# Cross-attention values by seven block products, with the context laid in another order

## The chip, the cores and the metric

The kernel runs on one core of one Trainium2 chip. The metric is the device time of one execution in microseconds (us). All data are float32.

## The reference, cut to what matters

The reference is one decoder layer: self attention, cross attention and a feed-forward network (FFN), each behind a layer norm and with a residual sum. There are 16 batches of 112 tokens with 512 features, 16 heads of 32, and a context of 375 tokens a batch.

```python
q = proj(hs, Wq, bq, S); k = proj(at, Wk, bk, T); v = proj(at, Wv, bv, T)
scores = clip(einsum('bhsd,bhtd->bhst', q, k) / sqrt(32), -50, 50)
scores = where(attend, scores, -10000.0); scores = clip(scores, -50, 50)
probs = softmax(scores); ctx = einsum('bhst,bhtd->bhsd', probs, v)
delta = clip(residual_scale, 0, 0.3) * (ctx @ Wo.T + bo); x = x + layernorm(delta)*gamma + beta
```

The change touches `k` and `v` of this cross attention: the products of the context (375 x 512) with two 512 x 512 weights.

## The kernel before, in words

`decoder_layer` (L1842) runs `finite_layer`, and after it `general_layer`, a slow version, only if a flag says that some value wasn't finite or in bounds. All below is in `finite_layer`.

**Stages.** Self attention (about 0 to 327 us), cross attention (327 to 826 us) and the FFN (826 to 1368 us). In the first two, a fixed chain of attention steps is interleaved with "pieces" of matrix products: a `Filler` `f` holds generators, each `yield` of a generator says how many us its matmuls are thought to take, and `f.fill(us)` issues pieces until so many us are used up. TensorE's order is the order in which the program issues its instructions (`manual_schedule`, L1610). The order on the other engines is made by a scheduler when the program is built.

**Cross attention.** The loop at L1699 goes over 16 batches `b`, and inside over three thirds (`kc`) of 125 context tokens. One `Cross.step` (L1238) does: 16 score matmuls (keys by queries), exponentials `e` on ScalarE, the weighting of the step before by its values (`weigh`), sums of `e` over the thirds on VectorE (`es`, L1280), and after the last third the sum over keys on TensorE (L941), four reciprocals and a product on VectorE (`divide`, L1284). Then `f.fill` issues pieces that prepare batch `b + 1`: its values, its keys, each second batch the queries of two batches (L870 ff., `xq`), and, once in four batches, output projections (`AfterCross`, L1188) whose finishing work is done on VectorE in the three batches that follow.

**Context, keys, values.** `Keys(b)` (L1066) loads one batch's context, features on partitions, as one DMA of 128 x 4 x 375 into a buffer `cT`. `sums` forms four block differences `kt` of it on VectorE. `keys` makes the keys by Strassen's scheme in Winograd's form: context and weights are cut into 2 x 2 blocks, and seven block products take the place of eight. The products share three PSUM banks and partly accumulate into each other; VectorE adds the results and the bias. `values` makes three tiles of 125 tokens x 512, each with four matmuls of 512 columns (`token_rows`, L887) and one copy on VectorE (L897). In the loop the two are interleaved: `mixed(values, keys, 2)`.

**Buffers.** PSUM tag `mm` has three banks in this stage: the products of values, keys, queries, projections and the key sums of `divide` rotate through them. The tag `big` has four buffers, shared by `cT` and `kT`; `v` has five; `w` (weights, `kt`, FFN blocks `f`) has eight; `row` has four, and holds among others the mask `mi` (L752) and the normalised rows `xn` (L789) at the start.

**The mask.** `mask_t` has 125 rows and 48 columns (batch by third). POOL loads it and makes scale and bias of the exponentials, `scl`, `nscl`, `bia`.

Of the kernel before, what the change touches and what calls it, by code (L numbers as in the profile page):

```python
# [12 lines left out]
I32 = mybir.dt.int32  # L13
U8 = mybir.dt.uint8
AF = mybir.ActivationFunctionType
ALU = mybir.AluOpType
AX = mybir.AxisListType

P = 128
# [7 lines left out]
KC = 3  # L27
# [570 lines left out]
def finite_layer(  # L598
# [47 lines left out]
    def weight(name):  # L646
        return wt.tile([P, C, D], F32, tag="w", name=name)
# [10 lines left out]
    def row(name):  # L658
        return ln.tile([P, D], F32, tag="row", name=name, bufs=4)
# [89 lines left out]
    nc.gpsimd.tensor_tensor(rs2, rs, rs, ALU.mult)  # L749


    mi = row("mi").bitcast(I32)[:KP, : B * KC]  # L752
    nc.gpsimd.dma_start(out=mi, in_=mask_t)
    scl, nscl, bia = (keep.tile([KP, B * KC], F32, name=n) for n in ("scl", "nscl", "bia"))
    nc.gpsimd.tensor_scalar(scl, mi, 0.5, SCALE, op0=ALU.is_gt, op1=ALU.mult)
    nc.gpsimd.tensor_scalar(nscl, scl, -1.0, None, op0=ALU.mult)
    nc.gpsimd.tensor_scalar(bia, mi, 0.5, 50.0, op0=ALU.is_gt, op1=ALU.mult)
    nc.gpsimd.tensor_scalar(bia, bia, -50.0, None, op0=ALU.add)

    dbk = keep.tile([P, 2], F32, name="dbk")  # L760
# [182 lines left out]
            )  # L943


    class Group:


# [7 lines left out]
        def keys(self):  # L956
            self.k = big("kT")
            yield from features(self.k, wk, xyT[:, :, ts(self.g, GT)], GT)
# [76 lines left out]
            f.drain()  # L1035

    def s_sums(s, a11, a12, a21, a22):
        for k, x0, x1, op in (
            (0, a21, a22, ALU.add),
            (1, s[:, 0], a11, ALU.subtract),
            (2, a11, a21, ALU.subtract),
            (3, a12, s[:, 1], ALU.subtract),  # L1050
        ):
            nc.vector.tensor_tensor(s[:, k], x0, x1, op)

    def t_sums(t, b11, b12, b21, b22):

        for k, x0, x1 in (
            (0, b12, b11),
            (1, b22, t[:, 0]),
            (2, b22, b12),
            (3, b21, t[:, 1]),  # L1060
        ):
            nc.vector.tensor_tensor(t[:, k], x0, x1, ALU.subtract)

    HK = (S2 + 1) // 2

    class Keys:  # L1066


        def __init__(self, b):
            self.b, self.v = b, []  # L1070
            self.c = big("cT")
            nc.sync.dma_start(out=self.c[:, :, :S2], in_=ctx_t[b])
            nc.gpsimd.memset(self.c[:, :, S2 : 2 * HK], 0.0)

        def sums(self):
            self.t = weight("kt").rearrange("p c n -> p (c n)")[:, : 8 * HK].rearrange(
                "p (s k n) -> p s k n", s=4, k=2
            )
            self.bs = [
                self.c[:, ts(d, 2), ts(k, HK)] for d in range(2) for k in range(2)  # L1080
            ]
            t_sums(self.t, *self.bs)

        def first_keys(self):
            self.k = big("kT")
            yield from features(self.k, xk, self.c[:, :, :S2], S2, bk)

        def keys(self):


            self.k = big("kT")
            c11, c12, c21, c22 = (
                self.k[:, ts(d, 2), ts(k, HK)] for d in range(2) for k in range(2)
            )
            b11, b12, b21, b22 = self.bs
            (a11, a12, a21, a22), s, t = xk_blocks, xks, self.t

            def bank():
                return psum("mm", [P, D])[:, : 2 * HK].rearrange("p (m n) -> p m n", m=2)

            def product(acc, lhs, rhs, first):
                for m in range(2):
                    for k in range(2):
                        nc.tensor.matmul(  # L1104
                            acc[:, m],
                            lhs[:, k, ts(m, P)],
                            rhs[:, k],
                            start=first and m == 0 and k == 0,
                            stop=k == 1,
                            skip_group_check=True,  # L1110
                        )
                return 1.28

            add, st = nc.vector.tensor_tensor, nc.vector.scalar_tensor_tensor
            a = bank()
            took = product(a, a11, b11, True)
            for m in range(2):
                nc.vector.tensor_scalar(
                    c21[:, m], a[:, m], bk[:, 2 + m : 3 + m], None, op0=ALU.add
                )  # L1120
            yield took
            b = bank()
            took = product(b, s[:, 1], t[:, 1], True)
            for m in range(2):
                st(
                    c12[:, m],
                    in0=b[:, m],
                    scalar=dbk[:, m : m + 1],
                    in1=c21[:, m],
                    op0=ALU.add,  # L1130
                    op1=ALU.add,
                )
            yield took
            took = product(a, a12, b21, False)
            for m in range(2):
                nc.vector.tensor_scalar(
                    c11[:, m], a[:, m], bk[:, m : m + 1], None, op0=ALU.add
                )
            yield took
            took = product(b, s[:, 2], t[:, 2], False)  # L1140
            add(c22, b, c21, ALU.add)
            yield took
            d = bank()
            took = product(d, s[:, 0], t[:, 0], True)
            add(c22, d, c22, ALU.add)
            yield took
            took = product(b, a22, t[:, 3], False)
            add(c21, b, c21, ALU.add)
            yield took
            took = product(d, s[:, 3], b22, False)  # L1150
            add(c12, d, c12, ALU.add)
            yield took

        def values(self, kcs=range(KC)):
            for kc in kcs:
                v = values("v")
                self.v.append(v)
                yield from token_rows(
                    v[:KP], xv, self.c[:, :, ts(kc, KP)], nc.vector.tensor_copy
                )  # L1160

    class Queries:

# [67 lines left out]
    class Cross:  # L1231
# [5 lines left out]

        def step(self, b, kc, q, keys, f, us):  # L1238
            scs = scores(
                lambda i, j: keys.k[ds(i * DH, DH), j, ts(kc, KP)],  # L1240
                lambda i, j: q[ds(i * DH, DH), j, ts(b % 2, S)],
                KP,
            )
            n = b * KC + kc
            late = self.late

            es = [(pair("es", "es", 3) if kc == 0 else pair("e"))[:KP] for _ in scs]
            self.late = (b, kc, keys.v[kc][:KP], es)
            for i, sc in enumerate(scs):
                nc.scalar.activation(  # L1250
                    es[i], sc, AF.Exp, scale=scl[:, n : n + 1], bias=bia[:, n : n + 1]
                )
            for i, sc in enumerate(scs):
                nc.scalar.activation(  # L1254
                    sc,
                    sc,
                    AF.Relu,
                    scale=nscl[:, n : n + 1],
                    bias=limit[:KP, :1],
                    accum_out=low[:KP, 2 * n + i : 2 * n + i + 1],  # L1260
                )
            self.weigh(late)
            for i in range(2):
                self.add(late, i)
            self.divide(late)
            f.fill(us)
# [10 lines left out]
        def add(self, late, i):  # L1277
            if late is not None and late[1] > 0:
                total = self.es[i][:KP]
                self.last = nc.vector.tensor_tensor(  # L1280
                    total, total, late[3][i][:KP], ALU.add
                ).ins

        def divide(self, late):  # L1284
            if late is not None and late[1] == KC - 1:
# [385 lines left out]
    for _ in w2_prep:  # L1671
# [6 lines left out]
    kv.append(Keys(0))  # L1678
    lay(11, 15.5, mixed(grp[3].values(range(GB)), n2[1].transposes(), 5))

    xks = weight("xks").rearrange("p c n -> p (c n)").rearrange(
        "p (s k n) -> p s k n", s=4, k=2
    )
    xk_blocks = [
        xk[:, ts(k, 2), ts(d, 2 * P)] for d in range(2) for k in range(2)
    ]
    s_sums(xks, *xk_blocks)
    lay(12, 10.5, after_self(whole[2], n2[2]))
    lay(13, 10, n2[2].ahead(False), kv[0].first_keys())
    kv.append(Keys(1))  # L1690
    lay(14, 12, mixed(kv[0].values(), n2[2].transposes(), 3))
    qs = [Queries(n) for n in range(B // 2)]
    lay(15, 9.5, qs[0].pieces(), output_bias())
# [5 lines left out]
    for b in range(B):  # L1699
# [16 lines left out]
        if b + 1 < B:  # L1716


            f.add(mixed(kv[b + 1].values(), kv[b + 1].keys(), 2))
            if b % 2:  # L1720
                queries = qs[(b + 1) // 2].pieces()
                us += 6.0
                if bl == 3 and g < 3:
                    n = n2[3] if g == 0 else n3[g - 1]
                    queries = mixed(queries, n.transposes(), 6)
                    us += 2.0
                f.add(queries)
# [170 lines left out]
```

## Time and profile before

| | us |
|---|---|
| three runs | 1371.20, 1369.81, 1370.17 (median 1370.17) |
| the profiled execution | 1369.86 |
| its span in the profile | 1368.1 |
| TensorE (PE) busy | 1347.5 |
| TensorE's weight loads (PEld) busy | 805.2 |
| VectorE (DVE) busy | 788.3 |
| ScalarE (ACT) busy | 462.0 |
| GpSimd (POOL) busy | 35.4 |

A line of a group names the source line, the engine, the operation, output<-inputs by the program's names, the shapes and the count; then busy time in us and the mean ns of one; then the idle time of the engine just before them and what ended it. A line of a timeline has start, length, engine, line, operation, names, count, and in brackets the idle time before it and who ended it. Matmuls are pipelined, and their ends are modelled: two that follow each other overlap in the profile, so what one costs is the distance between starts. One float32 matmul of the source appears as two records.

### The profile page before, as it was taken

What the parts mean: (1) busy time and instruction counts of PE and PEld (TensorE: products, weight loads), DVE (VectorE), ACT (ScalarE), POOL (GpSimd) and SP (SyncE); (2) the same over time, 40 slices, a digit from 0 to 9 for tenths busy, and PEclk for the clock granted to TensorE, in tenths of its full rate; (3) what the DMA queues carried; (4) which work ended last, traced back from release to release, by engine and by line L of the source; (5) the groups of instructions that cost most, each with busy time, mean ns of one, the idle gap of its engine ahead of it and who ended that gap; (6) DMA issues with size and microseconds to landing.
All of it is one profiled execution on the core that took longest, in us unless ns stands there. A gap on an engine that the chain in (4) does not pass through costs nothing.

```text
span 1368.1 us, 20027 instructions
## 1 busy us (share of the span) xinstructions
PE 1347.5 (98%) x8328; PEld 805.2 (59%) x8328; DVE 788.3 (58%) x1509; ACT 462.0 (34%) x901; POOL 35.4 (3%) x68
## 2 busy tenths in 40 slices
PE   8999999999999999999999999999999999999997
PEld 5555555556676767766777765544555555555554
DVE  3377987783645575547655567557654245554332
ACT  3355664553344435343445453201110011111000
POOL 2000001030000100000000000000000000000000
PEclk9999999999999999999999999999999999999999
DMA  9100002610000000000011011112031112322201
GB/s 319 52 1 16 17 15 86 245 54 1 23 24 24 31 24 23 24 24 24 24 39 39 25 48 32 46 31 62 31 123 62 47 61 69 93 65 89 93 0 56
DMA packets 59720, 74.02 MB, mean 54 GB/s; under 512 B 2641, under 2 KB 47713, under 8 KB 57317
## 3 DMA queue, kind: packets, MB, share of 16 engines
q1 hardware_dynamic: 57952, 69.44, 15.4%
q0 software_dynamic: 672, 1.62, 0.5%
q8 instruction: 67, 1.10, 0.3%
q10 hardware_dynamic: 996, 1.59, 0.3%
q14 instruction: 33, 0.26, 0.1%
HBM read 61.63 MB, written 11.01 MB: 53 GB/s over the span
## 4 chain that ended last, share of the span: by engine, by line
PE 91%; DVE 5%; ACT 1%; DMA 1%; issue 1%; POOL 0%; ACTq 0%; SPq 0%; DVEq 0%; POOLq 0%
PE mm L892 15%; PE gate L1462 12%; PE mm L874 10%; PE mm L1104 9%; PE ys L1462 7%; PE mm L903 7%; PE gate L1396 6%; PE mm L1462 5%; PE sc L919 5%; PE ys L930 4%; PE ys L1396 4%; PE mm L1396 3%; PE sc L1027 2%; PE mm L835 1%; PE mm L941 1%
## 5 line engine op out<-in xcount | busy, mean ns | idle before, releaser
L892 PE MATMUL mm<-xv,cT 128*125 128x512 f32 x384 | 178.6, 601 | 0.0
L1250 ACT ACTIVATE e<-sc,bia,scl 125x896 f32<-125x896 f32 x64 | 68.4, 1094 | 192.1 <-PE sc L919 192.1
L892 PEld LDWEIGHTS mm<-xv,cT 128*125 128x125 f32 x384 | 68.4, 187 | 75.5 <-issue 74.1
L1254 ACT ACTIVATE sc<-sc,limit,nscl 125x896 f32<-125x896 f32 x96 | 102.6, 1068 | 0.0
L1462 PE MATMUL gate<-t,f 128*128 128x448 f32 x256 | 101.4, 539 | 0.0
L1280 DVE TENSOR_TENSOR es<-es,e 125x896 f32<-125x896 f32 x64 | 68.4, 1089 | 52.5 <-ACT e L1250 52.5
L1396 PE MATMUL gate<-h,f 128*128 128x448 f32 x224 | 86.6, 539 | 0.0
L1462 PE MATMUL gate<-xyT,f 128*128 128x448 f32 x192 | 80.1, 540 | 0.0
L994 ACT ACTIVATE e<-sc,mx 112x112 f32<-112x112 f32 x256 | 64.4, 399 | 42.5 <-DVE mx L990 42.5
L1462 PE MATMUL ys<-t,f 128*128 128x448 f32 x192 | 77.4, 539 | 0.0
L1462 PEld LDWEIGHTS gate<-t,f 128*128 128x128 f32 x256 | 48.6, 190 | 47.6 <-issue 47.0
L1478 ACT COPY u<-gate 128x448 f32<-128x448 f32 x16 | 8.5, 531 | 182.3 <-PE gate L1462 109.4
L1104 PEld LDWEIGHTS mm<-kt,xks 128*128 128x128 f32 x360 | 59.0, 190 | 15.3 <-issue 14.9
L1396 PEld LDWEIGHTS gate<-h,f 128*128 128x128 f32 x224 | 42.5, 190 | 41.3 <-issue 40.9
L1292 DVE RECIPROCAL r<-mm 128x112 f32<-128x112 f32 x64 | 47.8, 810 | 30.8 <-PE mm L941 30.8
L1104 PE MATMUL mm<-kt,xks 128*128 128x188 f32 x360 | 63.5, 324 | 0.0
L989 DVE TENSOR_REDUCE mx<-sc 112x8 f32<-112x896 f32 x32 | 33.6, 1083 | 42.4 <-PE sc L919 42.4
L892 PE MATMUL mm<-wv,xyT 128*112 128x512 f32 x128 | 58.0, 596 | 0.0
L1462 PEld LDWEIGHTS ys<-t,f 128*128 128x128 f32 x192 | 36.5, 190 | 35.7 <-issue 35.5
L1408 DVE TENSOR_TENSOR h<-h,h 128x896 f32<-128x896 f32 x32 | 32.8, 1084 | 40.9 <-PE ys L1396 31.7
L1462 PEld LDWEIGHTS gate<-xyT,f 128*128 128x128 f32 x192 | 36.0, 190 | 34.4 <-issue 33.7
L919 PE MATMUL sc<-q,kT 32*125 32x112 f32 x1536 | 54.7, 279 | 0.0
(211 smaller groups left out, 2192.8 us busy)
## 6 DMA issues: line engine op xcount, KB each, us to landing
f<-in_f_w SPq DMA_DIRECT2D x64, 256.0 KB, 3.1
f<-blocks SPq DMA_DIRECT2D x14, 1024.0 KB, 4.8
cT<-in_ctx SPq DMA_DIRECT2D x16, 750.0 KB, 4.8
w<-in_f_w SPq DMA_DIRECT2D x4, 1024.0 KB, 10.3
blocks<-w SPq DMA_DIRECT2D x4, 1024.0 KB, 5.4
xr<-in_x SPq DMA_DIRECT2D x2, 1024.0 KB, 10.8
out_y<-o SPq DMA_DIRECT2D x8, 256.0 KB, 3.2
xr<-in_x SPq DMA_DIRECT2D x2, 768.0 KB, 15.7
```

What stands on the lines that cost most here:

```text
L874: nc.tensor.matmul(acc[:, :n], w[:, c, ts(j, P)], src[:, c, :], start=(c == 0), stop=(c == C - 1))
L892: nc.tensor.matmul(acc[:n, :], src[:, c, :], w[:, c, :], start=(c == 0), stop=(c == C - 1))
L903: nc.tensor.matmul(acc, xyT[:, c, ts(t, P)], w[:, c, :], start=(c == 0), stop=(c == C - 1))
L919: nc.tensor.matmul(views[i // 2][:, i % 2, j, :], k_of(i, j), q_of(i, j), start=True, stop=True)
L930: nc.tensor.matmul(y[ts(i, DH), j, :], v[:, HG * j + i, :], es[i // 2][:n, i % 2, j, :], start=first and j == 0, stop=last, skip_group_che ...
L994: nc.scalar.activation(e[:, i, j, :], sc[:, i, j, :], AF.Exp, scale=SCALE, bias=mx[:, i, j : j + 1],)
L1104: nc.tensor.matmul(acc[:, m], lhs[:, k, ts(m, P)], rhs[:, k], start=first and m == 0 and k == 0, stop=k == 1, skip_group_check=True,)
L1250: nc.scalar.activation(es[i], sc, AF.Exp, scale=scl[:, n : n + 1], bias=bia[:, n : n + 1])
L1254: nc.scalar.activation(sc, sc, AF.Relu, scale=nscl[:, n : n + 1], bias=limit[:KP, :1], accum_out=low[:KP, 2 * n + i : 2 * n + i + 1],)
L1280: self.last = nc.vector.tensor_tensor(total, total, late[3][i][:KP], ALU.add).ins
L1396: nc.tensor.matmul(banks[m][bank], o[:, c, ts(m, P)], t[:, c, :], start=first and c == 0, stop=c == UNITS - 1, skip_group_check=True,)
L1462: nc.tensor.matmul(bank, o[:, s, k, :], t[:, k, :], start=first and k == 0, stop=k == 1, skip_group_check=True,)
```

## The change

1. **Context in another order.** The load is split into five DMAs. Tokens 0 to 124 stand at columns 0 to 124, tokens 125 to 249 at columns 188 to 312, and the last 125 fill what is left of the two halves of 188 columns (63 and 62); the first 63 of these are laid a second time at the end (columns 375 to 437), so that each third is also one run of columns (`third`). The memset of the padding goes.
2. **Two thirds of the values by seven products** (`Seven.rows`): the tiles of tokens 0 to 249 come from seven products of two matmuls with 256 columns, with the weight's block sums `xvs` (made once) and the block sums `kt` that the keys use already. Each product has a bank; VectorE makes eight sums of 125 x 256. The last third stays a direct product, and is issued first.
3. **Keys with a bank for each product** (`Seven.biased`): the same seven products in another order, with no accumulation across products, and one more sum on VectorE. After them POOL copies 63 columns of the keys to the end of the tile (`whole`).
4. **Mask.** The mask is loaded a second time in two parts, into a second `row` buffer, for the order of the last third, and scale and bias of that third are made from it.
5. Batch 0 keeps direct keys (376 columns instead of 375) and direct values, from the new layout.

```diff
-    mi = row("mi").bitcast(I32)[:KP, : B * KC]
-    nc.gpsimd.dma_start(out=mi, in_=mask_t)
-    nc.gpsimd.tensor_scalar(scl, mi, 0.5, SCALE, op0=ALU.is_gt, op1=ALU.mult)
-    nc.gpsimd.tensor_scalar(bia, mi, 0.5, 50.0, op0=ALU.is_gt, op1=ALU.mult)
+    parted = (S2 + 1) // 2 - KP
+    for kcs, parts in (
+        (slice(0, KC), ((0, 0, KP),)),
+        (slice(KC - 1, KC), ((0, parted, KP - parted), (KP - parted, 0, parted))),
+    ):
+        mi = row("mi").bitcast(I32)[:KP, : B * KC]
+        for to, start, n in parts:
+            nc.gpsimd.dma_start(out=mi[ds(to, n)], in_=mask_t[ds(start, n)])
+        m, sc_, bi = (
+            t.rearrange("p (b k) -> p b k", k=KC)[:, :, kcs] for t in (mi, scl, bia)
+        )
+        nc.gpsimd.tensor_scalar(sc_, m, 0.5, SCALE, op0=ALU.is_gt, op1=ALU.mult)
+        nc.gpsimd.tensor_scalar(bi, m, 0.5, 50.0, op0=ALU.is_gt, op1=ALU.mult)
...
+        def biased(self, dst, src, t, bias, over):
...
+            acc = product(a11, b11)
+            for m in range(2):
+                nc.vector.tensor_scalar(
+                    c21[:, m], acc[:, m], bias[:, 2 + m : 3 + m], None, op0=ALU.add
+                )
+            yield took
+            add_over(c11, product(a12, b21), c21)
+            yield took
+            add(c12, product(s[:, 1], t[:, 1]), c21)
+            yield took
+            add(c22, product(s[:, 2], t[:, 2]), c12)
+            yield took
+            add(c21, product(a22, t[:, 3]), c22)
+            yield took
+            acc = product(s[:, 0], t[:, 0])
+            add(c22, acc, c22)
+            add(c12, acc, c12)
+            yield took
+            add_over(c12, product(s[:, 3], b22), c12)
+            yield took
+
+        def rows(self, dst, src, t):
...
+            for w, x, *sums in (
+                (a11, b11, (c21, None)),
+                (a12, b21, (c11, c21)),
+                (s[:, 1], t[:, 1], (c12, c21)),
+                (s[:, 2], t[:, 2], (c22, c12)),
+                (a22, t[:, 3], (c21, c22)),
+                (s[:, 0], t[:, 0], (c22, c22), (c12, c12)),
+                (s[:, 3], b22, (c12, c12)),
+            ):
+                acc = psum("mm", [P, D])[:n, : 2 * P]
+                for k in range(2):
+                    nc.tensor.matmul(acc, x[:, k, :n], w[:, k], start=k == 0, stop=k == 1)
+                for c, more in sums:
+                    if more is None:
+                        nc.vector.tensor_copy(c, acc)
+                    else:
+                        nc.vector.tensor_tensor(c, acc, more, ALU.add)
+                yield 0.9
...
-            nc.sync.dma_start(out=self.c[:, :, :S2], in_=ctx_t[b])
-            nc.gpsimd.memset(self.c[:, :, S2 : 2 * HK], 0.0)
+            self.x = self.c[:, :, : 2 * HK]
+            parted = HK - KP
+            for to, start, n in (
+                (0, 0, KP),
+                (KP, 2 * KP, parted),
+                (HK, KP, KP),
+                (HK + KP, 2 * KP + parted, KP - parted),
+                (S2, 2 * KP, parted),
+            ):
+                nc.sync.dma_start(
+                    out=self.c[:, :, ds(to, n)], in_=ctx_t[b][:, :, ds(start, n)]
+                )
+
+        @staticmethod
+        def third(ap, kc):
+            return ap[..., ds(min(kc, 1) * HK + max(kc - 1, 0) * KP, KP)]
+
+        def whole(self):
+            nc.gpsimd.tensor_copy(self.k[:, :, S2 : HK + 2 * KP], self.k[:, :, KP:HK])
...
+        def pieces(self):
             self.k = big("kT")
+            keys = xks.biased(self.k, self.x, self.t, bk, dbk)
+            self.v = [values("v") for _ in range(2)]
+            rows = xvs.rows(
+                [v[:KP].rearrange("p h r -> p (h r)") for v in self.v],
+                quarters(self.x),
+                self.t,
+            )
+            last = self.third_of_values(KC - 1)
+            for _ in range(2):
+                yield next(last)
+            for _ in range(7):
+                yield next(rows)
+                yield next(keys)
+            self.whole()
...
+    xvs = Seven("xvs", xv)
...
-            f.add(mixed(kv[b + 1].values(), kv[b + 1].keys(), 2))
+            f.add(kv[b + 1].pieces())
```

## The prediction

> **What bounds the kernel now.** I read the busy times first, then the busy times of the stretch of cross attention (326.6 to 826.0 us, columns: length, then busy time and count of PE, PEld, DVE, ACT, POOL, then clock, DMA share, GB/s).
>
> ```profile
> PE 1347.5 (98%) x8328; PEld 805.2 (59%) x8328; DVE 788.3 (58%) x1509; ACT 462.0 (34%) x901; POOL 35.4 (3%) x68
> ```
> ```profile
> 0.00:40.00 40.00, 33.73 (x155) 22.61 (x156) 15.61 (x61) 12.14 (x24) 8.97 (x30) 1.00 0.86 291
> 326.60:826.00 499.40, 497.48 (x4737) 350.28 (x4736) 291.90 (x537) 230.68 (x354) 6.92 (x18) 1.00 0.09 27
> ```
>
> TensorE leaves 1.9 of 499.4 us idle there, at a granted clock of 1.00, so this stretch is worth what its matmuls take. The mean of a group (592 to 601 ns for 512 columns) isn't that price: matmuls overlap. The pitch is. In the timeline of the weight loads, and in the chain's whole runs (start, length, count):
>
> ```profile
> 635.25 0.19 PEld L892 LDWEIGHTS mm<-xv,cT 128*125 128x125 f32 x1 [0.24 <-issue]
> 635.68 0.19 PEld L892 LDWEIGHTS mm<-xv,cT 128*125 128x125 f32 x1 [0.24 <-issue]
> ```
> ```profile
> 658.18 6.05 PE mm L874 x32
> ...
> 1021.97 6.01 PE mm L1396 x16
> ```
>
> One record of 512 columns comes each 0.429 us, one of 448 each 6.01/16 = 0.376, one of 224 each 6.05/32 = 0.189. The line through these is 0.833 ns a column plus 2.5 ns. It gives 0.216 for 256 columns, which lie between two measured widths. Every fp32 matmul of the source is two records (64 calls of 16 score matmuls are 1,536 plus 512 records).
>
> **The term on the path: the values.** For each of batches 1 to 15, two of three value tiles (8 matmuls, 16 records of 512) go, and seven products of 2 matmuls (28 records of 256) come. 16 x 0.429 = 6.87 us; 28 x 0.216 = 6.05. That is 0.82 a batch, **-12.3 us** in all. The keys keep 28 matmuls of 188 columns. Bounds: -12.9 (exactly 7/8 of the columns) to 0, should the pitch not hold.
>
> The trace speaks against this pitch nowhere. The Trainium skill does (TensorE: Matmul & The Clock Gate, "Back-to-back issue gap"): it measures streams at 81 ns for 128 columns and 131 for 512, so width costs little. As an estimate by that page, 256 columns cost 98/131 of 512, the new products 28 x 0.321 = 9.0 us, and the kernel would be 2.1 us a batch, 32 us in all, slower. The rows above, 0.189 at 224 and 0.429 at 512, don't agree with it.
>
> **What VectorE gets.** Durations by row: 0.42 for 128x256, 0.55 for 128x376, 0.41 for 128x188 (two in a row 0.73), 0.69 for a 125x512 copy.
>
> ```profile
> L1280 DVE TENSOR_TENSOR es<-es,e 125x896 f32<-125x896 f32 x63 | 67.3, 1089 | 51.5 <-ACT e L1250 51.5
> L1292 DVE RECIPROCAL r<-mm 128x112 f32<-128x112 f32 x60 | 44.8, 810 | 30.8 <-PE mm L941 30.8
> L1141 DVE TENSOR_TENSOR kT<-mm,kT 128x376 f32<-128x376 f32 x15 | 8.2, 547 | 5.2 <-PE mm L1104 5.2
> L1052 DVE TENSOR_TENSOR f<-f 128x256 f32<-128x256 f32 x8 | 3.0, 421 | 3.0 <-DMA f<-in_f_w 3.0
> ```
>
> A batch loses two copies (1.38) and gains eight 256-wide sums (3.4 alone, 2.9 in a row) and one 376-wide key sum (0.5): +2.0 to 2.5 us on 18.2, where a batch has some 31. So VectorE goes from 59% to about 67%: not the bound by its sum. What counts is **how soon it empties a bank**. The values and keys had 6 banks a batch out of 3; now 15 products take one each, about every 1.07 us (0.86 for rows, 1.28 for keys). A product waits when VectorE is more than two products (2.14 us) behind. In the trace of before nearly all evacuations start 0.04 to 0.7 us after their matmul, but behind the sums `es` or the reciprocals up to 2.5 us. Before, this cost little:
>
> ```profile
> 636.41 2.98 DVE L1292 RECIPROCAL r<-mm 128x112 f32<-128x112 f32 x4
> 639.30 0.63 DVE L897 COPY v<-mm 125x512 f32<-125x512 f32 x1
> 639.54 1.51 PE L1104 MATMUL mm<-cT,xk 128*128 128x188 f32 x8 [0.69 <-DVE r L1292]
> ```
>
> Here (batch 8 to 9) the sums of the softmax hold one of the three banks until the reciprocals end, 8.7 us after the scores began at 630.71, since finishing work on `xr` stood ahead of them. Matmuls covered 1.07 + 0.80 + 0.86 + six of 512 (5.3) = 8.0 us. After, the cover until a third bank is needed is one whole third (3.5) and one row product (0.86): 7.2 us. By batch:
>
> - 4 to 5 and 8 to 9, with finishing work ahead of the reciprocals in the changed program's order too: about 1.7 waited instead of 0.7 each, and 0.4 behind it: **+2.4**.
> - 13 to 14: the second block of FFN weights now takes the buffer of `xq`, whose last matmul ends just before the scores; 1.1 us of issues, 3.0 to land and 1.6 of block sums now come ahead of the reciprocals: they end 8.8 after the scores begin, plus what queued: **+1.7**.
> - Other boundaries: key sum 0.8, `kt` sums 2.1, reciprocals 3.0: 5.9 after the scores, within 7.2. **0**; if that cover is gone, each us is one on the path.
> - Inside batches, two pairs of `es` sums: the second waits for ScalarE up to 3.3 us after the scores, and runs 1.09; an evacuation behind it starts 4.4 late. Bounds 0 to 0.6 each, 0 to 18 in all; I take 0.15 a batch, nearest to the few waits of before: **+2.2**.
> - Gone: accumulating into a bank that VectorE had first to read (0.7 waited for L1141): **-0.7**.
>
> **The context in five pieces.** SyncE issues take 0.54, so the last leaves 2.2 us after the first; a 256 KB load lands in 3.0 to 3.1, a 750 KB one in 4.4 to 6.2. The last piece lands at 5.3 at best, 2.2 + 6.2 = 8.4 at worst. `kt` sums wait for all five and stand ahead of the reciprocals. In the six boundaries without query products there are 1.3 us of room, so the bounds are 0 and 6 x 1.8 = 11; nearest is the small load: **+1.0**. Cover: the third's matmuls.
>
> A 1,500 B row takes 75 ns of a DMA engine (6.2% of 16 x 39.7 us over 528 packets), a 512 B row 27 ns (17.2% of 16 x 21 us over 2,112, where FFN weights load). The Trainium skill (DMA: Bandwidth & Descriptors, "Specifications") says that below 512 B the engines read, modify and write; the new rows have 248 to 500 B. [...] No row of that kind is in this stretch of the trace.
>
> **The start.** The mask is read a second time for the last third. Two more POOL DMAs (0.56 each) lie in POOL's wait of 3.83 us for `rs`; two more operations don't.
>
> ```profile
> 15.08 0.37 POOL L757 TENSOR_SCALAR bia<-mi 125x48 f32<-125x48 int32 x1
> ...
> 15.49 0.56 DVE L792 TENSOR_SCALAR xn<-xr,seen,rstd 128x512 f32<-128x512 f32 x1 [1.04 <-POOL bia L757]
> ```
>
> The fourth `xn` waits for the buffer of `mi`, and TensorE for it (0.97 before L835, first query product at 17.50). A second `mi` takes another row buffer, released 0.42 + 0.37 later: **+0.8**; 0.7 if 16 columns are quicker, 2 if the pieces, issued 0.56 and 1.12 later than a load that took 6.7, land after POOL gets to them.
>
> **At nothing.** Block sums of `xv` (4 x 0.66): at 266.3 VectorE is idle for 5.24 us before the maxima at 271.50; without that, 2.6 at most. POOL's copy of 63 key columns (0.6 to 1.47, the rows for 128 and 512 columns) has two thirds of a batch before its reader and takes the place of a memset; without cover 15 x 1.5. Later context loads wait for that copy, made a batch before. One matmul fewer in the batch-0 keys: none, 376 columns for 375.
>
> **Sum.** -12.3 + 2.4 + 1.7 + 2.2 - 0.7 + 1.0 + 0.8 = -4.9 us. The profiled execution took 1369.86 (span 1368.1 and 1.8 around it), the median of three runs is 1370.17, 0.3 more. 1370.2 - 4.9 = **1365**.
>
> **Rivals.**
> - *The whole gain.* VectorE keeps up, because its mean load has 10 us a batch to spare; only the start and half of the boundaries cost: -12.3 + 0.8 = 1358.7. For it: lags of 0.04 us. Against it: the wait at 639.54 was there with more cover.
> - *Eaten up.* The wait inside batches is 0.5 instead of 0.15, or the context lands 1.5 us late at six boundaries (+5 to 9): 1369.5. For it: 7.4 us that VectorE waited for `cT` in before.
> - *Slower: three banks are too few.* VectorE's order is fixed. Each pair of `es` sums and the reciprocals hold evacuations 3 to 4 us, and 2.14 us of products cover it. At 0.5 us at each of three places in 15 batches this is 22.5 us, less the gain and with the start 1370.2 - 12.3 + 0.8 + 22.5 = 1381. It decides from 11.5/15 = 0.77 us a batch. For it: 15 products where 6 were. Against it: pairs are interleaved with evacuations in most batches, and the products behind them find banks emptied early.
> - *The change doesn't do what it says*, in that 256 columns cost more than half of 512: excluded in the main by 224 at 0.189.
>
> **Numbers.** My forecast 0.50 (1361 to 1368.5), the whole gain 0.17, eaten up 0.12, slower 0.21. About 0.2% (2.7 us) is what a measurement of this kernel can tell from none. A little of the forecast's own range lies within it: faster 0.62, same 0.17, slower 0.21. The range goes from 1357.5, below the whole gain, to 1373, and leaves the slow rival out.
>
> **What would show it.** In the changed profile: records of 256 columns 0.216 apart; the cross stretch some 6 us shorter; waits of TensorE for reciprocals of 1 to 2 us after batches 4, 8 and 13, few others on `mm`; the first query product near 18.3; `kt` sums seldom waiting over 1 us for `cT`. Wrong if every batch shows a wait of 0.5 us or more for v or kT sums, if the pitch is over 0.23, or if `cT` lands after 8 us.

## The result, and the profile after

| | before | after |
|---|---|---|
| median, five runs of each | 1370.84 us (1369.81 to 1371.61) | **1363.45 us** (1362.83 to 1364.87) |
| the profiled execution | 1369.86 | 1363.19 |
| its span | 1368.1 | 1361.4 |

The ratio is 0.9948, with a 95% interval of 0.9933 to 0.9962. Beside the last experiments the same two kernels gave 1371.20 and 1363.34 (0.9948, 0.9934 to 0.9961). The prediction was 1365.0, that is 4.9 us less; 7.4 us less were measured.

First the busy times, then the windows of the changed kernel (length; busy time and count of PE, PEld, DVE, ACT, POOL; granted clock, DMA share, GB/s):

```profile
PE 1337.2 (98%) x8508; PEld 841.2 (62%) x8508; DVE 822.2 (60%) x1618; ACT 462.2 (34%) x901; POOL 48.1 (4%) x72
```
```profile
0.00:40.00 40.00, 33.55 (x151) 22.76 (x152) 15.70 (x61) 11.91 (x24) 11.10 (x34) 1.00 0.86 291
326.60:820.00 493.40, 487.86 (x4945) 385.75 (x4946) 325.85 (x646) 231.81 (x357) 17.36 (x20) 1.00 0.13 31
499.00:502.00 3.00, 0.85 (x5) 0.45 (x4) 3.00 (x5) 0.00 (x0) 0.00 (x0) 1.00 0.00 0
502.00:504.00 2.00, 2.00 (x8) 2.00 (x9) 1.80 (x4) 0.76 (x2) 0.00 (x0) 0.55 0.00 0
504.00:506.00 2.00, 2.00 (x8) 1.69 (x7) 0.73 (x2) 0.00 (x0) 0.00 (x0) 0.59 0.00 0
```

TensorE is 10.3 us less busy. In cross attention it now stands idle for 5.5 us where it was 1.9, with VectorE at 66% instead of 58%. The waits of TensorE in this stretch (total in us, count, longest), first in the kernel before, then in the changed one, and behind them the changed kernel's chain across the boundary from batch 4 to 5 (start, length, what):

```profile
PE mm L1104 <- DVE r L1292: 1.1, 2, 0.7
PE mm L1104 <- DVE kT L1141: 0.7, 1, 0.7
```
```profile
PE mm L1013 <- issue: 5.2, 3, 2.1
PE ys L940 <- ACT eT L1165: 0.7, 1, 0.7
```
```profile
494.89 0.38 PE mm L951 x4
495.27 3.63 PE mm L902 x8
498.89 0.88 PE mm L1073 x4
499.77 2.13 issue
501.90 2.55 PE mm L1013 x8
504.46 1.50 PE mm L1073 x4
505.96 1.27 PE mm L1013 x8
507.24 0.86 PE mm L1073 x4
```

Three things are in these lines. Four records of 256 columns take 0.86 us: 0.215 each. All of TensorE's new idle time lies in three waits, put down to "issue", since the trace names no releaser. And after the first of them the same products take 2.55 and 1.50 us instead of 1.27 and 0.86: the windows show a granted clock (the share of full speed that TensorE was given) of 0.55 and 0.59 there; by the trace's clock record it is half speed from 502.22 us on, for 3.41 us. Who ended the wait is seen in the timeline of all engines:

```profile
498.15 0.75 DVE L1299 SCALAR_TENSOR_TENSOR xr<-d,rstd,xr 128x512 f32<-128x512 f32 x1
...
498.82 2.98 DVE L1370 RECIPROCAL r<-mm 128x112 f32<-128x112 f32 x4
501.72 0.63 DVE L907 COPY v<-mm 125x512 f32<-125x512 f32 x1
501.87 0.83 PEld L1013 LDWEIGHTS mm<-cT,xk 128*128 128x128 f32 x4 [2.52 <-issue]
501.90 0.99 PE L1013 MATMUL mm<-cT,xk 128*128 128x188 f32 x3 [2.15 <-issue]
```

The key product starts 0.1 us after the fourth reciprocal (498.82 + 2.98): it takes the bank of the key sums, and the finishing work on `xr` stood ahead.

**A ledger of the stretch.** From the trace I take as a wait what lies between two starts on TensorE beyond the pitch of the first record (0.833 ns a column and 2.5 ns), where it is more than 0.13 us; the column for the half clock has the same excess while the clock was half. From the first scores of cross attention to the start of the last 16 score matmuls:

| kernel | length | waits | half clock | rest |
|---|---|---|---|---|
| before | 496.33 | 2.87 (0.83, 0.24, 0.60, 0.15, 0.85, 0.20) | 0 | 493.46 |
| after | 488.29 | 5.70 (2.31, 1.91, 1.48) | 1.56 | 481.03 |
| direct values (experiment 1) | 494.64 | 2.08 (1.13, 0.95) | 0 | 492.56 |
| all losses taken out (experiment 8) | 480.69 | 0 | 0 | 480.69 |

Ahead of the stretch the first query product starts at 18.67 instead of 17.50 us (+1.17). From the first self-attention scores to the first of cross attention it is 277.15 before and 277.19 after; from the start of the last scores to TensorE's end 538.12 both times.

### The profile page after: what moved, and what is told of

It reads as the page before. It is cut to its first block, busy times and chain, and to the rows that moved or that the text cites. A ratio compares the mean times of both kernels' runs of the same rounds, so it can differ in the third digit from the quotient of the medians.

```text
span 1361.4 us, 20699 instructions
## 1 busy us (share of the span) xinstructions
PE 1337.2 (98%) x8508; PEld 841.2 (62%) x8508; DVE 822.2 (60%) x1618; ACT 462.2 (34%) x901; POOL 48.1 (4%) x72
## 3 DMA queue, kind: packets, MB, share of 16 engines
q8 instruction: 69, 1.13, 0.3%
## 4 chain that ended last, share of the span: by engine, by line
PE 94%; DVE 3%; issue 1%; ACT 1%; DMA 1%; POOL 0%; ACTq 0%; POOLq 0%
PE gate L1540 12%; PE mm L884 10%; PE mm L1013 10%; PE mm L902 9%; PE ys L1540 7%; PE mm L1073 7%; PE mm L913 7%; PE gate L1474 6%; PE mm L1540 5%; PE sc L929 5%; PE ys L940 4%; PE ys L1474 4%; PE mm L1474 3%; PE sc L1163 2%; PE mm L845 1%; PE mm L951 1%
## 5 line engine op out<-in xcount | busy, mean ns | idle before, releaser
L902 PE MATMUL mm<-xv,cT 128*125 128x512 f32 x144 | 66.4, 603 | 0.0
L929 PEld LDWEIGHTS sc<-q,kT 32*125 32x125 f32 x1536 | 46.2, 183 | 15.3 <-issue 15.3
```

The source lines that it names most:

```text
L902: nc.tensor.matmul(acc[:n, :], src[:, c, :], w[:, c, :], start=(c == 0), stop=(c == C - 1))
L929: nc.tensor.matmul(views[i // 2][:, i % 2, j, :], k_of(i, j), q_of(i, j), start=True, stop=True)
```

## The experiments

My theory after the result: the values' matmuls give the predicted gain, and what is lost are single waits for a bank at three boundaries, each set by what stands ahead of the reciprocals on VectorE, and the start. The rivals: the gain comes from another part of the change; or VectorE as a whole is late, so that a wait taken away returns elsewhere.

**1. Direct values, all else as changed.**

```diff
-            for _ in range(7):
-                yield next(rows)
-                yield next(keys)
+            yield from mixed(self.values(), keys, 2)
```

> All three value tiles by direct products again (24 records of 512 columns become 48 a batch... that is 16 x 0.429 us in place of 28 x 0.216 us for batches 1 to 15); context order, five-piece loads, two mask reads and keys with a bank each stay. Theory: the gain is the matmul time of the values, 0.82 us a batch, and what is lost are three waits for a bank at the batch boundaries 4-5, 8-9 and 13-14 (2.31, 1.91, 1.48 us, and 1.56 us at half clock behind the first). Direct values give 0.85 us more cover at each of the three: 1363.45 + 12.3 - 3 x 0.85 - 1.56 = 1371.6 us; the start stays at 18.67 us. Rival: the gain comes from the keys' banks or from the new order, and the values' products cost VectorE and TensorE what they save: 1363 to 1366 us.

(The count in its first bracket is muddled; the sum beside it is meant.) Measured: 1370.51 us, 1.1 below the theory's figure, 0.9997 of before (0.9988 to 1.0006). The waits are 1.13 and 0.95, the third is gone. Without waits the stretch takes 492.56 here and 481.03 in the changed kernel: the values' products are worth 11.5 us (11.9 against experiment 8), 0.77 to 0.79 a batch. The rival falls: without them the change gains nothing.

**2. Finishing work behind xyT.**

```diff
-                nc.vector.scalar_tensor_tensor(
+                self.last = nc.vector.scalar_tensor_tensor(
                     xyT[:, :, ts(b, S)],
...
-                )
+                ).ins
```

> The finishing work on xr is queued behind xyT of the same boundary, not behind the last sum of es: it no longer stands ahead of the reciprocals. Theory: the waits at 4-5 and 8-9 last until the reciprocals end and are there because of this work alone; without them 2.31 + 1.91 us and the 1.56 us at half clock go: 1357.7 us (1357.4 to 1358.5). Rival: VectorE has as much to do as before, so the work now holds the evacuations behind it, and the wait returns a few products later: 1360.5 to 1363 us. Second rival: the third value tile's copy or the context's key sums are late too: 1363 us, no change.

Measured: 1361.70 us (0.9934, 0.9920 to 0.9948). Both waits ahead of the reciprocals are gone, and 1.22 and 1.21 came back six products later; the first rival named it. In the timeline of this kernel:

```profile
506.44 1.42 DVE L1299 SCALAR_TENSOR_TENSOR xr<-d,rstd,xr 128x512 f32<-128x512 f32 x2
...
507.77 1.28 DVE L776 BATCH_NORM_STATS2 st<-xr 128x6 f32<-128x512 f32 x2
...
508.97 0.41 DVE L1078 TENSOR_TENSOR v<-mm,v 125x256 f32<-125x256 f32 x1
...
509.43 0.43 PE L1013 MATMUL mm<-kt,xks 128*128 128x188 f32 x1 [1.05 <-DVE v L1078]
```

The evacuation L1078 waited behind the finishing work, and the product for its bank.

**3. The mask in buffers of its own.**

```diff
-        mi = row("mi").bitcast(I32)[:KP, : B * KC]
+        mi = evp.tile([KP, B * KC], I32, tag="mi", name="mi", bufs=2)
```

> Both reads of the mask go to buffers of their own, none to a row buffer. Theory: the fourth xn (in this program the third too) waits only for POOL's use of the row buffer; without it the transposes follow each other, the first query product starts at 16.2 to 17.4 us in place of 18.67, and all behind it moves as a whole: 1361.1 to 1362.2 us. Rival: the late landing of x (the statistics ended 1.1 us later than in the kernel before) sets the start: first query product at 18.2 us or later, 1363.0 us or more.

Measured: 1360.44 us (0.9928, 0.9915 to 0.9942). The first query product starts at 17.52: 1.15 earlier, but not at 16.2 to 17.4, and the median is below the 1361.1 to 1362.2 that was expected. The `xn` no longer wait for POOL; what is left is the end of the statistics, late as in the kernel after, and ScalarE's four copies. With both, in experiments 7 and 8, it is 16.96 and 16.91. The rest of the 3.0 us is half-clock time (none behind the 2.31 us here, by where that wait happened to fall; see the last section) and 0.26 less at the third wait. So by this profile about 1.15 us are the buffers' doing.

**4 and 6. The sums of f(0,1) later.** Both load only f(0,0) at the old place:

```diff
-            ready.update({(0, i): load_blocks(0, i) for i in range(2)})
+            ready[0, 0] = load_blocks(0, 0)
```

Experiment 4 moves the other call behind the first third of batch 14, in the text alone; experiment 6 puts it a batch later and ties it behind a VectorE instruction:

```diff
+            if b == B - 2 and kc == 0:
+                ready[0, 1] = load_blocks(0, 1)
```
```diff
+            if b == B - 1 and kc == 0:
+                with tc.issue_after(cross.last):
+                    ready[0, 1] = load_blocks(0, 1)
```

> The second block of FFN weights, f(0,1), is loaded and its block sums issued after the first third of batch 14, so they stand behind the reciprocals of batch 13. Theory: the wait of 1.48 us at 785.38 us goes and nothing takes its place: 1362.0 us. Rival: the load then lies beside the context and the sums hold evacuations inside batch 14: 0.5 us comes back or more, 1362.5 to 1363.5 us.

> Block sums of f(0,1) queued behind the last es sum of batch 14, a batch later (in the run before they had stayed ahead of the reciprocals of batch 13: moved in the program's text, not in VectorE's order). Theory: the reciprocals of batch 13 start 2.5 us or more earlier, the wait of 1.48 us goes and nothing takes its place (the boundary behind batch 14 has 8.1 us of room): 1362.0 us, with single executions 1.6 us either way. Rival: the wait is set by something else at this boundary (its weights' landing, the third tile's copy): 1363.4 us with 1 us or more left at the same product.

Measured: 1363.05 (0.9939, 0.9925 to 0.9952) and 1362.99 us (0.9937, 0.9923 to 0.9950). Experiment 4 didn't move what it meant to: the scheduler put the sums at the same place. Timeline of 4, then of 6:

```profile
782.46 1.55 DVE L969 TENSOR_TENSOR f<-f 128x256 f32<-128x256 f32 x4 [6.30 <-DMA f<-in_f_w]
...
783.94 2.98 DVE L1370 RECIPROCAL r<-mm 128x112 f32<-128x112 f32 x4
...
787.02 0.40 PE L1013 MATMUL mm<-cT,xk 128*128 128x188 f32 x1 [1.25 <-issue]
```
```profile
781.48 2.99 DVE L1370 RECIPROCAL r<-mm 128x112 f32<-128x112 f32 x4 [0.56 <-PE mm L951]
...
785.71 0.32 PE L1013 MATMUL mm<-cT,xk 128*128 128x188 f32 x1
```

In 6 the wait is gone. In its median this hardly shows: half-clock time of 1.5 us at the boundary from 4 to 5 and 1.7 at the start lie in the profiled execution, and single runs go from 1359.26 to 1363.89.

**5. Finishing work by the piece.**

```diff
...
-                        nc.vector.tensor_tensor(c, acc, more, ALU.add)
+                        behind[0] = nc.vector.tensor_tensor(c, acc, more, ALU.add).ins
...
-                with tc.issue_after(cross.last):
-                    for _ in range(2):
+                with tc.issue_after(behind[0]):
+                    for _ in range(1 if bl == 1 else 2):
                         next(finish, None)
         f.drain()
+        if bl == 0 and g < 3:
+            next(finish)
```

> The finishing work is laid out by the piece: the rstd chain as soon as the projections are done, then one or two pieces a third, each behind that third's last evacuation of values. Theory: the waits came from where this work stood, not from how much VectorE has to do (65% of the stretch); in the idle time before the es sums it costs nothing: the waits of 2.31 and 1.91 us go, the half-clock time behind the first goes where it came, and none returns: 1358.3 us (1357.4 to 1359.5). Rival: VectorE is simply full around these boundaries and the wait returns elsewhere, as behind xyT, where 1.22 and 1.21 us returned: 1361 to 1362 us.

Measured: 1361.14 us (0.9928, 0.9914 to 0.9942), single runs from 1359.27 to 1366.54; the profile is of the slowest of these. The waits at both boundaries are gone. New ones of 0.63 and 2.15 us stand in batches 6 and 10.

**7 and 8. All together.** Experiment 7 is 3, 5 and 6 in one; 8 changes one expression in it.

```diff
-                    for _ in range(1 if bl == 1 else 2):
+                    for _ in range(2 if bl == 2 and kc == 2 else 1):
```

> Mask buffers apart, finishing work spread, sums of f(0,1) behind batch 14, all on the changed kernel. Theory: the losses are separate and add: 1363.45 - 1.15 (start) - 4.2 (two boundaries) - 1.5 (third) - 0.8 (half-clock time, in about half of the executions) = 1355.8 us (1354.5 to 1357), and TensorE waits nowhere in the stretch of cross attention. Rival: what is freed at one place is waited for at the next, as VectorE is late by its load: 1358 to 1360 us.

> As the combined kernel, with the finishing work one piece a third, so that the last xr update and the next rstd chain (4.5 us together) no longer stand in one third. Theory: a third takes up to about 2.3 us of this work without a wait, since VectorE idles before the es sums; the waits of 0.63 and 2.16 us in batches 6 and 10 go and nothing returns: TensorE waits under 0.3 us in all in the stretch of cross attention behind its first score, 1358.2 - 2.8 - 0.7 (half-clock time in half of the executions) = 1354.8 us (1353.5 to 1356). Rival: another pair of pieces collides: over 1357 us.

Measured: 1358.24 us (0.9909, 0.9894 to 0.9924), then **1354.95 us** (0.9882, 0.9867 to 0.9897; 1354.45 to 1355.70). In 7 the new wait is as in 5; its timeline shows what collides:

```profile
665.72 0.69 DVE L776 BATCH_NORM_STATS2 st<-xr 128x6 f32<-128x512 f32 x1
...
666.67 0.17 DVE L784 TENSOR_SCALAR rstd<-seen 128x4 f32<-128x4 f32 x1
...
668.34 1.09 DVE L1360 TENSOR_TENSOR es<-es,e 125x896 f32<-125x896 f32 x1
...
671.35 0.48 PE L1073 MATMUL mm<-xvs,kt 128*125 128x256 f32 x1 [1.99 <-DVE kT L1023]
```

The last `xr` update and the chain of small `rstd` steps stood in one third, ahead of the `es` sums and of the key evacuations behind those. One piece a third, and TensorE has no wait left; waits and window of experiment 8:

```profile
PE ys L940 <- ACT eT L1165: 0.7, 1, 0.7
```
```profile
326.60:815.00 488.40, 488.40 (x4988) 385.41 (x4980) 329.14 (x649) 233.24 (x358) 17.88 (x20) 1.00 0.13 31
```

VectorE is busy for 67% of this, as much as where waits were. So its load was not the cause; its order was.

**9. The reciprocals twice.**

```diff
-                for c in range(C):
+                for c in (*range(C), *range(C)):
                     nc.vector.reciprocal(r[:, c], sums[:, c])
```

> Each of the four reciprocals of a batch is done twice with the same result: 2.98 us more of VectorE while the sums hold a bank. Theory: a boundary pays what goes beyond its room. In the changed kernel's trace nine boundaries have 1.24 us between the last reciprocal and the product that takes the bank, three have none, three (4, 8 and 15 as the following batch's number less one: those with 512-column products behind) have 3.8 us or more: 9 x (2.98 - 1.15) + 3 x 2.98 = 25.4 us, with half-clock time of 0 to 1.6 us behind each wait above 2 us: 1389 to 1394 us. Rival: room is a matter of VectorE's mean load, 65% here, and 3 us in some 31 of a batch are taken up mostly: under 10 us, 1372 us. Second rival: the delay goes on to evacuations inside the batches: more than 40 us, over 1404 us.

Measured: 1399.18 us (1.0212, 1.0197 to 1.0228). Waits of TensorE:

```profile
PE mm L1013 <- issue: 27.5, 12, 5.0
PE ys L940 <- ACT eT L1165: 0.7, 1, 0.7
```

Nine waits of 1.70 to 1.72 (1.83 expected), three of 5.16, 4.76 and 4.17 (2.7 to 2.85 more than they were), as the theory has it, and 0.25 more in all inside batches: both rivals fall. The total is above the theory's for two things that I left out: 4.4 us at the end, where the first weighting of batch 15 waits for the reciprocals of batch 14 (2.6) and the first FFN products for those of batch 15 (1.8), and half-clock time of 5.2 us behind the three long waits.

**10. Two banks.**

```diff
-    banks_of = {"mm": 3, "ys": 1}
+    banks_of = {"mm": 2, "ys": 1}
```

> Two banks for products in place of three in attention, all else as in the changed kernel. Theory: a product waits where VectorE is more than one product behind in place of two. By the changed kernel's trace 99 products of the cross stretch would start before their bank is free, by 56 us together, less what each wait gives back to those behind it: 20 to 56 us more in this stretch. Rival: evacuations mostly follow their product at once, and only the three boundaries are late: under 15 us more there. Self attention loses a bank too, so the stretch is compared alone.

Measured: 1416.61 us (1.0329, 1.0313 to 1.0344). The stretch is 38.0 us longer than in the changed kernel, within the theory's range; 37 waits over 0.25 us sum to 28.5. The three largest groups that the trace names:

```profile
PE mm L1073 <- issue: 6.0, 3, 2.4
PE mm L1013 <- DVE kT L1019: 4.3, 10, 0.7
PE mm L1013 <- DVE kT L1023: 3.6, 5, 0.7
```

The rival of the prediction, too few banks, thus has a price; it shows one bank below.

**11. Keys with a bank each, alone, on the kernel before.** Its `keys` gets the products and sums of `Seven.biased` in their order; the rest is the kernel before.

> The kernel before with one part of the change alone: each key product in a bank of its own, no accumulation in a bank that has been read. Theory: the waits of the accumulation (0.83, 0.24 and 0.15 us in the trace of before) go, those for a free bank at the boundaries 4-5 and 8-9 (0.60, 0.85) grow to about 1.1: 1370.2 us, no difference from before that can be measured. Rival: seven banks a batch in place of three make products wait inside the batches: 1373 us or more. Second rival: a good part of the gain is here: 1368 us or less.

Measured: 1371.23 us (1.0001, 0.9992 to 1.0010). In its trace the accumulation's waits are gone, 0.96, 0.84 and 0.62 stand for a bank, and the stretch is 495.07, 1.26 less than before: the part does what it says, and it is too small to show in the median.

**12. The changed kernel once more**, unaltered.

> The changed kernel once more, unaltered, beside the others. Theory: the waits of 2.31, 1.91 and about 1.4 us come again at the same products, since the order on the engines is fixed; half-clock time behind the 2.31 us, and behind the wait of 2.37 us at 142 us, comes or doesn't by execution: 1362 to 1364.5 us. Rival: the half clock belongs to this program: it is there again behind the first wait and nowhere else.

Measured: 1363.34 us (0.9948, 0.9934 to 0.9961), waits of 2.31, 1.92 and 1.33 at the same products, and half clock behind the first again (1.60 us). That it isn't bound to this program is seen in the last section.

## Why the prediction was right or wrong

| step | predicted | measured |
|---|---|---|
| values | -12.3 | -11.5 to -11.9 |
| boundaries 4-5 and 8-9 | +2.4 | +2.8 in waits, +1.6 at half clock |
| 13-14 | +1.7 | +1.5 |
| inside batches | +2.2 | 0 |
| key accumulation | -0.7 | -1.2 in waits, -0.9 in gaps |
| context in five DMAs | +1.0 | 0 |
| start | +0.8 | +1.2 |
| sum | -4.9 | -6.7 (profiled executions) |

With a wait of 0.20 of before that has gone, the measured column sums to -6.7 as rounded (-6.9 from the unrounded lengths). The profiled executions differ by 6.7: behind TensorE's last matmul the changed kernel takes 0.15 us longer, and 0.04 lies in self attention.

That 1365 came so near is in part luck. The terms that came out dearer than predicted (values, the first two boundaries with their half clock, the start) make some 3 us, those that came out cheaper (inside batches, key accumulation, the context, the third boundary, the wait of 0.20) make 5.0.

- **The values: right.** The pitch is 0.215 to 0.216, and width costs in proportion. The estimate from the Trainium skill's page (TensorE: Matmul & The Clock Gate, "Back-to-back issue gap") of 32 us more is refuted by the chain's 0.86 us for four records. What takes the 0.4 to 0.8 us that are missing from -12.3 was not found.
- **The three boundaries: right in place and cause, the size mixed.** The places, the cause (finishing work and the FFN's sums ahead of the reciprocals) and the third's 1.5 us were as the prediction had them. It took 1.7 us of wait at each of the first two, where before had 0.7, and 0.4 behind them; 2.31 and 1.91 came, and nothing behind. The cover was right: from the first score of the batch to the product that needs the bank TensorE had 7.12 and 7.13 us of work (7.2 predicted). Mis-sized was the end of the reciprocals. The prediction kept the 8.7 us after the scores that it had read at boundary 8-9 of before (8.43 at 4-5); now they end 9.34 and 8.93 us after them. The batch 5 scores begin here, and the reciprocals shown above end at 501.80:

```profile
492.47 1.14 PE L929 MATMUL sc<-q,kT 32*125 32x112 f32 x32
```

At the third boundary they end 8.51 us after the scores (8.8 predicted). Half clock behind a wait wasn't in the prediction at all.
- **Inside batches: the step that failed.** 0.15 a batch was taken for evacuations behind the second `es` sum, because waits of before looked like it. None came in 15 batches. The room is thin, as in the changed kernel's timeline:

```profile
419.57 1.09 DVE L1360 TENSOR_TENSOR es<-es,e 125x896 f32<-125x896 f32 x1 [0.27 <-ACT e L1330]
...
420.58 0.75 DVE L1078 TENSOR_TENSOR v<-mm,v 125x256 f32<-125x256 f32 x2
...
421.55 0.32 PE L1013 MATMUL mm<-cT,xks 128*128 128x188 f32 x1
```

The product at 421.55 takes the bank that L1078 empties at 421.33: 0.22 us early. A bound from the order of VectorE's queue could have shown this; a mean wait could not. With two banks, or 2.3 us of finishing work more in one third, the wait is there.
- **The context: the bounds held (the last piece lands 6.0 to 7.2 us after the first issue in the 14 loads where the trace has it), the price didn't.** VectorE waits for it at five boundaries, 8.2 us in all and up to 2.1 at one, more than the "seldom over 1 us" of the prediction, but nine boundaries still have 1.24 us of room behind the reciprocals, which experiment 9 used up to within 0.1. What the Trainium skill says of rows below 512 B (DMA: Bandwidth & Descriptors, "Specifications") brought no cost on the path: a 250 KB piece takes 3.8 us to land (median), a 256 KB load of FFN weights 3.1. In the packets of three of the new loads (at 485, 520 and 652 us) a row of 248 or 252 B took 18 ns of a DMA engine and one of 500 B 27 (medians), where a 512 B row of FFN weights took 27 before: a short row cost more by the byte, but not more by the row.
- **Key accumulation and the start: right in sign, small in size.** The prediction counted one wait of 0.7; there were three (1.2 in all), and short gaps with them. Experiment 11 shows the gaps too: its stretch less its waits is 492.65, 0.8 below the 493.46 of before. At the start the third `xn` waits as well (for the first mask's buffer), and POOL's `scl` took 0.92 instead of 0.42 us beside VectorE's `xn`. In nine profiles with this mask code the first query product starts at 18.33 to 18.89.
- **The rivals.** "Eaten up" needed 0.5 us inside each batch or a late context; neither came. The slow one (three banks too few) needed 0.77 us a batch; there were 0.38 (5.70 in 15), and experiment 10 shows that it comes with two. "The whole gain" (1358.7) didn't come in the kernel as changed; with VectorE's order mended, experiment 8 goes below it, as it also takes out waits that the kernel before had.
- **At nothing: right.** Self attention and FFN kept their lengths to 0.04 us; POOL's 16 copies (0.39 to 1.32 us each) are waited for by nobody.

## What to carry to other kernels

Where the matmul bounds, price fewer columns by the pitch between starts, and then look for the price of the change not in the load of the evacuating engine but in its order: list, for each product, when the bank it takes is emptied, and see which long items (reciprocals, norms, sums that wait for a DMA) stand ahead. Small finishing work belongs in pieces where that engine idles anyway; laid in one block it moves the wait instead of taking it away. And see in the built queue that a moved instruction has moved: where a scheduler orders an engine, its place in the text may mean nothing.

## What the runs showed of the hardware that was not expected

**Half clock after short waits.** After a wait of TensorE the granted clock can fall to half. In the clock records of the 14 profiles here, up to the last matmul, it does so for 3.413 us at a time, twice for 6.827, and within one trace the starts of all such stretches, with the one behind the last matmul, are whole multiples of 3.413 us apart: in the changed kernel 502.216 and 1355.548, which is 250 times. So time is cut into windows that run on by themselves; where they lie against the program differs from trace to trace.

What decides is how long TensorE stands idle within one window, not how long a wait is. I laid these windows over the traces and summed in each what lies beyond the pitch. Of the 5,508 that began at full clock from 9 us on, 20 held 2.12 us or more of idle time, and the clock was half in the next window behind all 20. 5,484 held less than 2.06, and it was half behind none. Of four between (2.07 to 2.11) it was half behind one. Such a window costs TensorE 1.4 to 1.8 us more than the wait.

So the same wait costs more or less by where it falls. The 2.31 us of boundary 4-5 lay in one window in four of five profiles and had the half clock behind it; in experiment 3 it lay 2.11 and 0.20 in two, and had not. Waits of 1.70 to 1.92 us never reach the sum alone. One kernel's executions scatter by a few us with it: of experiment 4's runs that of 1360.72 us has a mean granted clock of 0.999, that of 1364.95 one of 0.995. All this is read from the traces; no experiment moved a wait against the windows.

The Trainium skill (TensorE: Matmul & The Clock Gate, "What's actually happening") gives an idle window of some 3.4 us that runs freely, and the spacing of 3.413 us agrees. Its table "Why this matters for your kernels" warns of gaps above some 3 us; here 2.1 us of idle time in one window were enough.
